# Masked graph attention with nodes on the partitions, and 32x32 squares crossed inside SBUF

## The chip, the cores and the metric

The kernel runs on one core of a Trainium2 chip. The metric is the device time of one execution, in microseconds (us). The kernel before takes 4419.53 us, the median of 3 runs (4417.87 to 4420.16 us). Engines are named as in the profile: PE is the matrix engine (PEld its weight loads), DVE the vector engine, ACT the activation engine, POOL the general one, SP the engine whose queue issues nearly all DMAs.

## The reference

There are 32 independent graphs. Each has x of 512 nodes by 256 features, and all share one adjacency matrix `adj` (512x512, about 0.8% ones). Four layers follow each other, each of the form `x = x + layer(relu(layernorm(x)), adj)`:

- Layer 0: a matrix 256->512, an attention without mask over 512 features, a matrix 512->256, then **masked attention** over 256 features, with ELUs and residuals between.
- Layer 1: **masked attention** over 256 features; the mask also holds the diagonal.
- Layer 2: ordinary multi-head attention (MHA), 8 heads of 32 features, masked, then two layer norms and two 256x256 matrices.
- Layer 3: **masked attention** with 4 heads of 64 features.

The masked attention of layers 0, 1 and 3 is, cut to what matters:

```python
f1 = h @ a[:F];  f2 = h @ a[F:]                  # one number per node
e = leaky_relu(f1[:, None] + f2[None, :], 0.2)    # (512, 512)
e = where(adj > 0, e, -9e15)
out = elu(softmax(e, axis=1) @ h)
```

So one graph needs six 512x512 masked tables of this kind (layer 0: one, layer 1: one, layer 3: four) and eight of the MHA's kind.

## The kernel before, in words

All data are fp32. A [512, 256] array lies in SBUF as [128 partitions, 4, 256]; such a "cell" is 4 KB a partition. The program is not written in the order in which it runs. For each graph, `Graph` records operations (`op`, `transfer`) with an engine, a planned length and the buffers read and written. `Plan.order` then schedules all graphs' operations in a list: at each step it takes the engine that can start first, and there the operation with the smallest due time. Due times come from `PERIOD`, `CLOSE` and the list `SHIFTS`, one entry for each operation counted from the graph's end. Up to `IN_FLIGHT = 6` graphs are open at once. Buffers (32 cells, 7 rows, 48 DRAM pages, 12 DRAM sheets, 8 PSUM banks) are given out by the same list. The result is one fixed order for each engine, and one for the SP queue, which issues every DMA of the steady state: a DMA whose input is late holds up the DMAs behind it.

The parts that matter here:

- **`gat_probabilities` (L776)** makes one masked table with the *sources* on the partitions, so that PE can use it as it is. For each table: `rows_ps` (L714, the PE work on L720) spreads a column of node numbers over all partitions by four 128x128 transposes into a PSUM bank. This happens three times (f2, w, f1). DVE takes the greatest masked f2 of each node (four of L791); four short POOL operations (L806 to L809) make w from it; ACT copies w's row out of PSUM (L730); POOL adds the mask to it in two halves (L821); DVE takes the greater of f1 and a term and adds (four of L832); ACT takes the exponential (four of L840).
- **`lonely` and `spread` (L846, L867)** give nodes without a neighbour the mean of all nodes: POOL sums, one PE product with a matrix of ones (L859), an ACT copy (L863), a POOL product (L870).
- **`attended` (L918)** multiplies a table with the node features (PE, L927) and divides by the row sums on DVE (L944 to L951).
- **`layer3` (L1450)** builds four tables, sums them over sources with POOL (L1484, L1488) and PE (L1523), multiplies with PE (L1502), turns the results and the sums back (L1539), and adds the lonely nodes' mean on POOL (L1572).
- **`mha` (L1329)** already has its nodes on the partitions. Its products (L1347), mask and maximum (L1367), exponentials with their sums (L1378) make tables that must be transposed. DVE turns every 32x32 square in place (L1386). Then the squares change places: one DMA of 1 MB writes them to a DRAM sheet (L1391) and four DMAs of 256 KB, each to 32 partitions, read them back (L1399). PE reads the result in runs of 32 numbers (L1412). Table and crossed table are each a `Quad`, four neighbouring cells.
- **`turned_round` (L631)** transposes a layer's normalized input the same way (two DVE operations on L636, then L615 and L622 through a DRAM page); layers 0 and 2 use it. **`transposed` (L647)** does it on PE with eight transposes (L655) and two ACT copies (L663); layers 1 and 3 use it, and the second half of layer 2.

Of the kernel before, what the change touches and what calls it, by code (L numbers as in the profile page):

```python
# [9 lines left out]
FP = mybir.dt.float32  # L10
I32 = mybir.dt.int32
BF = mybir.dt.bfloat16
# [24 lines left out]
TERMS = 3  # L37
MOST = 40.0

FLOOR = -(2.0**60)  # L40
TINY = 1e-30
# [3 lines left out]
CELL = NC * (C + 5)  # L45
ROW = N + 10
SMALL = 320
BUFFERS = {"cell": 32, "row": 7, "page": 48, "sheet": 12}
# [6 lines left out]
PERIOD = 50.7  # L55
CLOSE = 1.0

SHIFTS = (
    72, 50, 37, 26, 40, 30, 9, 57, 9, 9, 9, 9, 50, 27, -10, -39, 3, -6, 21, -19, -30, -122,
    -182, -23, -9, -33, 39, 5, -2, 1, -49, 1, 1, 0, -66, 1, 1, 1, 1, -16, 1, -38, -1, -71, -1,  # L60
    0, -23, 1, 2, -22, 1, 3, 1, -103, 1, 5, 1, -19, 1, 1, 19, 1, -26, 1, -3, 1, 1, 1, 14, 5, 0,
    1, 1, -10, 1, -2, 0, 0, 0, 1, 0, -1, 0, -1, 6, 0, -115, 19, 0, 7, -25, -6, 0, -32, -35, 0,
    68, 0, 35, 0, 93, -3, 2, 24, -51, 18, -11, 0, -7, 1, -75, 1, 1, 55, 0, 26, -26, 4, 3, 0,
    -39, -1, -162, -3, -56, -2, -13, 1, -20, -2, -37, -87, -26, -9, -7, -1, -27, -9, -52, -40,
    6, -52, -18, 0, -6, -4, 2, -5, -23, -88, 0, -14, -42, 12, -11, -1, -2, 6, -7, -10, -1, -49,
    -29, -3, -1, -23, 2, 0, -84, 10, -16, -46, -3, 7, 7, -17, 0, 0, 0, 0, -18, 0, 4, 144, 2, 0,
    -3, 0, -7, 2, -24, 27, -28, 31, -92, 47, -25, -10, 1, 0, -3, 0, 109, 0, -1, -75, -1, 0, 0,
    -3, 0, -7, -45, 0, 41, -1, 2, -7, 69, -15, -49, -3, -3, 0, 22, -97, -17, 4, -12, -9, 4, -53,
    -11, -1, -1, -5, 17, 5, 72, 47, 46, 74, 146, -16, -51, 41, -3, -13, -15, 2, 0, 1, 49, -18,
    -5, 30, 3, 4, 0, 0, -1, 0, 18, 14, -12, -32, 78, -1, 37, -82, -4, 7, -6, 0, 9, -3, -12, 9,  # L70
    0, -70, 20, 0, -10, 0, -1, 0, 23, 0, 0, -33, -10, 28, 83, 95, 37, 17, 76, -5, -36, -119,
    -25, -1, 92, 3, 0, 2, -3, 0, -24, 1, 0, -10, -5, -3, -36, -2, -46, -24, -68, 25, -10, -11,
    -13, -5, -2, -29, -22, -1, -1, -13, -2, 3, 14, 0, 0, 0, 28, 7, -83, -101, 7, 46, -9, -54,
    -46, 44, -24, 99, -5, -1, 0, 0, 75, 0, 0, 0, -10, 0, 1, 6, 0, 14, 0, 23, 13, -17, 53, 6, 87,
    -7, -16, 7, 3, 5, -1, -71, -87, 15, -12, 0, 11, 0, 0, 0, 8, 0, 0, -9, -8, 0, 23, 0, 0, -80,
    2, 0, 18, 0, 0, -3, 0, 0, 105, -13, -36, -11, -81, -30, -85, -143, -51, -24, -71, -29, -116,
    -48, -84, -82, -187, -154, -123, -175, -94, -43, -87, -62, 6, -91, -111, -160, -332, -388,
    -421, -351, -608, -395, -425, -396, -421, -341, -408, -335, -348, -464, -413, -372, -375,
    -378, -330, -297, -285, -312, -291, -315, -190, -199, -193, -90, -130, -236, -99, 76, -225,
    -189, -251, -299, -395, -387, -220, -242, -187, -183, -124, -28, -137, -109, -189, -108,  # L80
    -163, -117, -33, -55, -60, -125, -183, -244, -216, -176, -221, -264, -255, -199, -296, -271,
    -259, -434, -424, -521, -444, -340, -233, -214, -298, -180, -115, -52, -68, -145, -240,
    -205, -240, -241, -326, -236, -241, -474, -309, -46, -175, -128, -162, -177, -202, -326,
    -320, -212, -315, -229, -218, -238, -255, -252, -253, -294, -281, -196, -99, -190, 0, -59,
    -31, 0, -31, 3, -6, 2, 0, 2, -13, 0, 0, 0, 0, 16, 0, 141, -61, 0, 0, 0, -77, -2, -15, -29,
    -84, -35, -22, -60, -26, -26, -15, -26, -229, -39, -46, -103, -103, -16, -128, -41, -4, -61,
    -7, 35, -2, -9, 23, 3, 2, -22, -73, 5, -12, 2, 2, 2, -6, 2, 2, -5, 3, 2, 64, -18, 3, -11, 3,
    -24, 2, 2, 2, 3, 3, 42, 3, 1, 3, -26, 1, 3, -80, 17, -29, 27, -4, 3, 3, 3, 3, 3, 3, 3, -42,
    3, 0, -10, -36, -8, -69, -213, 23, -10, -20, 25, 26, 33, -18, 68, -12, -53, 17, 91, 94, 5,
    111, 25, 57, 164,  # L90
# [46 lines left out]
class Quad(Buffer):  # L137

    width = 4

    def __init__(self, *shape):
        super().__init__("cell", *shape)
# [266 lines left out]
def adj_preln_kernel(  # L409
# [35 lines left out]
    ident_bf = const.tile([P, P], BF, name="ident_bf")  # L445
    nc.vector.tensor_copy(ident_bf, ident)
    ones = const.tile([P, P], FP, name="ones")
# [5 lines left out]
    tiny = const.tile([P, NC], FP, name="tiny")  # L453
    nc.vector.memset(tiny, TINY)
# [20 lines left out]
    def row(v, name):  # L475
# [6 lines left out]
    mask_biasT = const.tile([P, NC, N], BF, name="mask_biasT")  # L482
    self_biasT = const.tile([P, NC, N], BF, name="self_biasT")
    alone = const.tile([P, NC], FP, name="alone")
# [5 lines left out]
    hand_sb = weights(W_hand, "hand_sb", TERMS)  # L490
    l1_sb = weights(W_1, "l1_sb", TERMS)
# [4 lines left out]
    l3_sb = weights(W_3, "l3_sb", TERMS * GAT_HEADS)  # L496
# [10 lines left out]
    none = const.tile([P, NC], FP, name="none")  # L507
# [8 lines left out]
    cells = work.tile([P, BUFFERS["cell"] * CELL], FP, name="cells")  # L516
    Buffer.at["cell"] = [cells[:, k * CELL :] for k in range(BUFFERS["cell"])]
    Buffer.at["bank"] = banks
    Buffer.at["sheet"] = [
        pages.tile([P, QUAD], FP, name=f"sheet{k}") for k in range(BUFFERS["sheet"])  # L520
    ]
    Buffer.at["page"] = [
        pages.tile([P, PAGE], FP, name=f"page{k}") for k in range(BUFFERS["page"])
    ]
    smalls = [work.tile([P, SMALL], FP, name=f"smalls{k}") for k in range(IN_FLIGHT)]
    masked = work.tile([P, N], FP, name="masked")
# [14 lines left out]
    out_v = out.rearrange("b (c p) f -> b p c f", p=P)  # L541

    class Graph:
# [129 lines left out]
        def channels_first(self, src, w, cols, dst, bias=None):  # L673

            nk = w.shape[1]
            for m in range(2 * len(dst)):
# [12 lines left out]

                def emit(m=m, mm=mm, d=d, i=i):  # L690
                    if bias is None:
                        act.activation(d[:, i, :], mm.ap, AF.Copy)
                    else:
                        act.activation(d[:, i, :], mm.ap, AF.Relu, bias=bias[:, m : m + 1])
# [81 lines left out]
        def gat_probabilities(self, holder, term, n, bias, biasT, own=False, after=()):  # L776

            f2_ps = self.rows_ps(holder, lambda c: term(0)[:, c : c + 1], after)

            top = self.small(f"top{n}", NC)
            w = self.small(f"w{n}", NC)
            for c in range(NC):
                self.op(
                    "dve", 0.77, [f2_ps, held("mask", c)], [top],  # L790
                    lambda c=c: dve.tensor_tensor_reduce(  # L791
                        masked, f2_ps.ap, bias[:, c, :], 1.0 - ALPHA, FLOOR,
                        op0=ALU.add, op1=ALU.max, accum_out=top[:, c : c + 1],
                    ),
                )
            if own:
                self.op(
                    "dve", 0.25, [top, *holder], [top],
                    lambda: dve.scalar_tensor_tensor(
                        top.ap, term(2), -1.0, top.ap, op0=ALU.mult, op1=ALU.max  # L800
                    ),
                )

            def emit():
                t = top.ap
                pool.tensor_add(w.ap, t, term(1))  # L806
                pool.tensor_scalar(w.ap, w.ap, 0.0, -1.0, op0=ALU.max, op1=ALU.mult)
                pool.tensor_scalar(t, t, -ALPHA / (1.0 - ALPHA), None, op0=ALU.mult)
                pool.tensor_add(w.ap, w.ap, t)  # L809

            self.op("pool", 1.0, [top, *holder], [top, w], emit)
            p = [Buffer("cell", 2, N) for _ in range(2)]
            w_row = self.row_of(w, lambda c: w[:, c : c + 1], p)

            def bias_key(half):
                return [("selfT" if own else "maskT", 2 * half + i) for i in range(2)]

            for half in range(2):
                self.op(
                    "pool", 2.17, [w_row, bias_key(half)], [p[half]],  # L820
                    lambda half=half: pool.tensor_add(  # L821
                        p[half].ap,
                        biasT[:, 2 * half : 2 * half + 2, :],
                        w_row[:, None, :].to_broadcast([P, 2, N]),
                    ),
                )
            f1_ps = self.rows_ps(holder, lambda c: term(1)[:, c : c + 1], [w_row])
            for j in range(NC):
                ph, i = p[j // 2], j % 2
                self.op(  # L830
                    "dve", 0.75, [f1_ps, *holder, ph.part(i)], [ph.part(i)],
                    lambda j=j, ph=ph, i=i: dve.scalar_tensor_tensor(  # L832
                        ph[:, i, :], f1_ps.ap, term(2)[:, j : j + 1],
                        ph[:, i, :],
# [813 lines left out]
```

## Time and profile before

| quantity | value |
|---|---|
| median of the runs | 4419.53 us |
| the profiled execution's own time | 4422.42 us |
| its span, first to last instruction | 4420.6 us |
| mean granted PE clock | 0.979 |
| PE busy over the span | 4170.8 us (94%) |
| DVE, POOL, ACT busy | 3662.7, 3034.1, 2924.3 us |
| DMA moved, mean busy share of the 16 DMA engines | 867.22 MB, 66.4% on SP's queue |

The profile has several views. The page gives busy times over the span. A table by stage gives the same for a stretch of time: for each engine its busy us and, in brackets, the number of its instructions, then PE's granted clock, the DMA engines' busy share and the GB/s moved. The groups give for one line of the code the shapes, the count, the busy us, the mean ns of one instruction, and the idle time before them with what ended it. The timeline lists instructions in order: start, us, engine, line, shapes, count. Instructions of one engine overlap at their ends, so the time that one more instruction costs is the distance between starts, a little less than its duration.

### The profile page before, as it was taken

How to read it: one execution, taken by the hardware profiler on the slowest of the kernel's cores; microseconds unless marked ns; L12 is line 12 of the kernel's file. 1: busy time of each engine (PE TensorE's matmuls, PEld its weight loads, DVE VectorE, ACT ScalarE, POOL GpSimd, SP SyncE). 2: the span in 40 equal slices, each digit the busy share in tenths (PEclk: the TensorE clock that was granted, in tenths of full speed). 3: DMA queues.
4: the chain of work that ended last, by engine and by line, in shares of the span. 5: the costliest groups of instructions: out<-in, count | busy, mean ns of one | idle time of the engine just before them, and what ended most of it. 6: DMA issues, size and time to landing. Idle time of an engine off the chain costs nothing. (4 is left out here: it accounts for less than half of the span.)

```text
span 4420.6 us, 69315 instructions
## 1 busy us (share of the span) xinstructions
PE 4170.8 (94%) x21648; PEld 2583.3 (58%) x21648; DVE 3662.7 (83%) x9016; ACT 2924.3 (66%) x6309; POOL 3034.1 (69%) x3119
## 2 busy tenths in 40 slices
PE   6999999999999999999999999999999999999765
PEld 3656556665566666566666556666656666655332
DVE  3577888888888888888888888888889888888873
ACT  2556666777676667667667767666766766676653
POOL 1424766777776677776677777667777766777677
PEclk9999999999999999999999999999999999999877
DMA  3287667766767766766777667677667677766760
GB/s 121 84 226 218 187 190 220 218 202 181 215 199 211 224 200 201 204 204 194 222 215 204 201 200 211 194 224 210 205 205 206 192 217 219 201 200 186 231 175 29
DMA packets 441504, 867.22 MB, mean 196 GB/s; under 512 B 35248, under 2 KB 119728, under 8 KB 441136
## 3 DMA queue, kind: packets, MB, share of 16 engines
q1 hardware_dynamic: 439520, 862.78, 66.4%
q8 instruction: 173, 2.83, 0.3%
q14 instruction: 195, 1.60, 0.1%
q10 hardware_dynamic: 1616, 0.01, 0.0%
HBM read 443.23 MB, written 419.43 MB: 195 GB/s over the span
## 5 line engine op out<-in xcount | busy, mean ns | idle before, releaser
L1386 DVE STREAM_TRANSPOSE cells<-cells 128x512 f32<-128x512 f32 x1024 | 702.4, 698 | 148.8 <-ACT cells L1378 148.5
L1378 ACT ACTIVATE cells<-cells,smalls 128x512 f32<-128x512 f32 x1024 | 736.1, 719 | 114.0 <-DVE smalls L1367 105.8
L1367 DVE CUSTOM_DVE_ANT_0 cells<-bank,mask_bias 128x512 f32<-128x512 f32 x1024 | 686.9, 674 | 21.6 <-PE bank L1347 20.6
L821 POOL TENSOR_TENSOR cells<-mask_biasT,row 128x1024 f32<-128x1024 bf16 x320 | 682.3, 2155 | 16.2 <-ACT row L730 16.2
L791 DVE CUSTOM_DVE_ANT_0 masked<-bank,mask_bias 128x512 f32<-128x512 f32 x768 | 520.5, 678 | 71.1 <-PE bank L720 64.7
L683 PE MATMUL bank<-cells,mlp_sb 128*128 128x512 f32 x1024 | 473.1, 600 | 19.8 <-DMA cells<-page 13.2
L704 PE MATMUL bank<-fc_sb,cells 128*128 128x256 f32 (+1 forms) x2048 | 474.7, 381 | 1.5 <-DVE smalls L1367 0.8
L927 PE MATMUL bank<-cells 128*128 128x260 f32 x2048 | 465.1, 383 | 1.1 <-ACT cells L840 0.9
L603 ACT ACTIVATE cells<-cells,smalls 128x256 f32<-128x256 f32 x768 | 408.1, 592 | 74.7 <-POOL smalls L596 49.7
L1159 PE MATMUL bank<-cells 128*128 128x512 f32 x1024 | 450.9, 597 | 0.0
L927 PEld LDWEIGHTS bank<-cells 128*128 128x128 f32 x2048 | 387.9, 190 | 87.1 <-issue 24.9
L840 ACT ACTIVATE cells<-cells,smalls 128x512 f32<-128x512 f32 x512 | 348.5, 726 | 114.7 <-DVE cells L832 114.6
L704 PEld LDWEIGHTS bank<-fc_sb,cells 128*128 128x128 f32 x2048 | 376.9, 189 | 76.5 <-DVE cells L1442 19.0
L586 DVE BATCH_NORM_STATS2 smalls<-cells 128x6 f32<-128x256 f32 x768 | 311.3, 405 | 110.4 <-POOL cells L1222 101.3
L883 ACT ACTIVATE cells<-cells 128x512 f32<-128x512 f32 (+1 forms) x256 | 188.1, 735 | 292.9 <-DVE cells L946 111.3
L832 DVE SCALAR_TENSOR_TENSOR cells<-bank,smalls,cells 128x512 f32<-128x512 f32 x512 | 354.1, 740 | 30.5 <-POOL cells L821 27.0
L720 PEld LDWEIGHTS bank<-ident,smalls 128*128 128x128 f32 x2176 | 254.3, 141 | 212.6 <-issue 84.2
L720 PE MATMUL bank<-ident,smalls 128*128 128x128 f32 x2176 | 325.9, 284 | 54.2 <-POOL smalls L809 30.0
L1159 PEld LDWEIGHTS bank<-cells 128*128 128x128 f32 x1024 | 194.1, 193 | 230.2 <-issue 228.7
L1484 POOL TENSOR_TENSOR cells<-cells 128x1024 f32<-128x1024 f32 x128 | 302.3, 2372 | 19.2 <-PE bank L1502 8.4
L683 PEld LDWEIGHTS bank<-cells,mlp_sb 128*128 128x128 f32 x1024 | 186.0, 191 | 218.5 <-issue 170.3
L1347 PE MATMUL bank<-cells 32*128 32x512 f32 x2048 | 305.8, 644 | 5.7 <-DVE smalls L1367 4.8
(141 smaller groups left out, 8503.9 us busy)
## 6 DMA issues: line engine op xcount, KB each, us to landing
sheet<-cells SPq DMA_DIRECT2D x256, 1024.0 KB, 5.3
cells<-sheet SPq DMA_DIRECT2D x1024, 256.0 KB, 5.4
page<-cells SPq DMA_DIRECT2D x256, 512.0 KB, 3.4
cells<-page SPq DMA_DIRECT2D x192, 512.0 KB, 6.1
cells<-in_x_dram SPq DMA_DIRECT2D x64, 512.0 KB, 7.3
cells<-page SPq DMA_DIRECT2D x256, 128.0 KB, 2.9
out_dram<-cells SPq DMA_DIRECT2D x32, 512.0 KB, 5.4
mlp_sb<-in_L_gnn_mlp_w_dram SPq DMA_DIRECT2D x2, 512.0 KB, 6.7
```

Source lines behind the costliest of these rows:

```text
L603: lambda c=c: act.activation(xn[:, c, :], src[:, c, :], func, bias=off[:, c : c + 1], scale=rstd[:, c : c + 1],),
L683: lambda k=k, s=s, i=i, m=m, mm=mm: pe.matmul(mm.ap, w[:, k, cols + m * P : cols + (m + 1) * P], s.rows(i), start=(k == 0), stop=(k == nk ...
L704: pe.matmul(mm[:, :n], src[k // 2].nodes(k % 2, c), w[:, k, cols : cols + n], start=(k == 0), stop=(k == nk - 1),)
L720: pe.transpose(bc[:, c * P : (c + 1) * P], col(c).to_broadcast([P, P]), ident)
L791: lambda c=c: dve.tensor_tensor_reduce(masked, f2_ps.ap, bias[:, c, :], 1.0 - ALPHA, FLOOR, op0=ALU.add, op1=ALU.max, accum_out=top[:, c : ...
L821: lambda half=half: pool.tensor_add(p[half].ap, biasT[:, 2 * half : 2 * half + 2, :], w_row[:, None, :].to_broadcast([P, 2, N]),),
L832: lambda j=j, ph=ph, i=i: dve.scalar_tensor_tensor(ph[:, i, :], f1_ps.ap, term(2)[:, j : j + 1], ph[:, i, :], op0=ALU.max, op1=ALU.add,),
L927: pe.matmul(mm[:, :w1], p[j // 2][:, j % 2, c * P : (c + 1) * P], v[:, j, :], start=(j == 0), stop=(j == NC - 1),)
L1159: pe.matmul(mm.ap, h1[jh][:, i, m * P : (m + 1) * P], p[jh][:, i, :], start=(jh + i == 0), stop=(jh + i == 2),)
L1367: dve.tensor_tensor_reduce(tile(), sc[h].ap.rearrange("p (j f) -> p j f", j=NC), mask_bias[:, c, :].rearrange("p (j f) -> p j f", j=NC), - ...
L1378: lambda h=h, c=c, tile=tile: act.activation(tile(), tile(), AF.Exp, scale=-1.0, bias=low[:, c, h : h + 1], accum_out=sums[:, c, h : h + 1],),
L1386: dve.transpose(squared, squared)
```

## The change

All masked tables are now made with the *targets* on the partitions, as the MHA's are, and turned by DVE and DMA:

- `masked_probabilities` takes the place of `gat_probabilities`. One spread row for each table instead of three. DVE adds the mask and takes the maximum, writing the table itself. One POOL addition and two small ACT operations make the shift. ACT applies the leaky slope as one instruction (`Prelu` with a bias), then the exponential; in layer 3 the exponential also gives the row sums. DVE turns the squares.
- `squares_crossed` moves each of the 16 blocks of squares with a DMA of its own from SBUF to SBUF, 128 KB (layer 3, and MHA in the same manner) or 64 KB (layers 0 and 1), each from 32 partitions to 32 partitions. Sheets in DRAM are gone.
- Layers 1 and 3 use `turned_round`. The nodes then come in an order by squares; the mask table is kept in that order, ACT writes r2T of layer 0 in that order, POOL copies it back to the plain one, and layer 3 fetches its residual and stores its result by quarters.
- `lonely`, `spread` and POOL's sums of layer 3 are gone; the divisions of `attended` become a DVE reciprocal and an ACT scaling.
- Quads get 5 buffers of their own beside 16 cells; rows go from 7 to 3. `PERIOD`, `CLOSE` and `SHIFTS` have other values.

```diff
-BUFFERS = {"cell": 32, "row": 7, "page": 48, "sheet": 12}
+BUFFERS = {"quad": 5, "cell": 16, "row": 3, "page": 48}
-PERIOD = 50.7
-CLOSE = 1.0
+PERIOD = 46.6
+CLOSE = 0.96
...
+        def masked_probabilities(self, holder, far, near, n, table, p, tile, parts, sums=None):
+            f2_ps = self.square_row(holder, far, [p])
...
+            for c in range(NC):
+                self.op("dve", 0.77, ...,
+                    lambda c=c: dve.tensor_tensor_reduce(
+                        tile(c), f2_ps.ap..., bias[:, c, :]..., 1.0, LOWEST,
+                        op0=ALU.add, op1=ALU.max, accum_out=top[:, c : c + 1]))
+            self.op("pool", 0.35, ..., lambda: pool.tensor_add(top.ap, top.ap, near()))
+            def emit():
+                act.activation(m.ap, top.ap, AF.Prelu, alpha=ALPHA)
+                act.activation(m.ap, m.ap, AF.Copy, scale=-1.0)
+            self.op("act", 0.45, [top], [m], emit)
+            for c in range(NC):
+                self.op("act", 0.72, ..., lambda c=c: act.activation(
+                    tile(c), tile(c), AF.Prelu, bias=near()[:, c : c + 1], alpha=ALPHA))
+            for c in range(NC):
+                ... act.activation(tile(c), tile(c), AF.Exp, bias=m[:, c : c + 1], **out)
+                ... dve.transpose(squared, squared)
...
+        def squares_crossed(self, src, dst, read, write, kbytes):
+            for turn in range(squares):
+                for l in range(squares):
+                    to = (l + turn) % squares
+                    ... nc.sync.dma_start(
+                            dst(slice(to * SQUARE, (to + 1) * SQUARE), l),
+                            src(slice(l * SQUARE, (l + 1) * SQUARE), to))
+                    self.transfer([read], write(l, to), kbytes, emit, True)
...
         def attended(self, p, v, y):
-                        dve.reciprocal(rinv.ap, mm[:, C + TERMS : w1])
-                        dve.tensor_mul(y[:, c, :], mm[:, :C], rinv.ap.to_broadcast([P, C]))
+                    lambda mm=mm, rinv=rinv: dve.reciprocal(rinv.ap, mm[:, C + PAIR : w1]),
+                    ... act.activation(y[:, c, :], mm[:, :C], AF.Copy, scale=rinv.ap)
...
         def layer0(self):
-            self.channels_first(yT, mlp2_sb, 0, [r2T], bias=mlp2_bc)
+            self.channels_first(yT, mlp2_sb, 0, [r2T], bias=mlp2_bc, squares=True)
+            rows = Buffer("cell", KC, N)
+                ... pool.tensor_copy(rows[:, k, :]..., r2T[:, k, :]...)
+            q = self.masked_attention(h2, (mask_square, "square"), 1)
-            self.spread(self.lonely(h2, self.W1), z)
...
         def layer1(self):
-            hT = self.transposed(xn)
+            hT = self.turned_round(xn)
...
         def mha(self, g, qT, kT, v, y):
-                    self.transfer([parts], [[(sheet, c % 2)]], 1024, ...)
-                    for to in range(squares):
-                        self.transfer([[(sheet, c % 2)]], [[(pT, c % 2, to)]], 256, emit, True)
+                for turn in range(squares):
+                    for l in range(squares):
+                        to = (l + turn) % squares
+                        self.transfer([squared], [[(pT, l, to)]], 128, emit, True)
...
         def layer3(self):
-            hT = self.transposed(xn)
+            hT = self.turned_round(xn)
...
-                    self.op("pool", 2.4, p, [halves], ... pool.tensor_add ...)
-                    self.op("pool", 1.27, [halves], [total.part(i)], ... pool.tensor_add ...)
+                    self.masked_probabilities(...)
+                self.squares_crossed(..., 128)
-            self.op("pe", 0.94, sums, [acc, r], emit)
-            back = turned(r, [])
...
-            self.transfer([res], [], 512, lambda: nc.sync.dma_start(out_v[i], res.ap))
+            for q in range(P // SQUARE):
+                self.transfer([res], [], 128, lambda q=q: nc.sync.dma_start(
+                    rows_v[q], res[q * SQUARE : (q + 1) * SQUARE]))
```

In the MHA the 16 transfers of a pair of blocks wait for all eight tables of the pair; before, the sheet of each block left as soon as its four tables were done.

## The prediction

> **What bounds the kernel now.** I read the table by stage first: start, one stretch of the middle, end.
>
> ```profile
> core 0: us, PE busy (x) PEld busy (x) DVE busy (x) ACT busy (x) POOL busy (x), PEclk, DMA share, GB/s
> 0.00:110.00 110.00, 70.94 (x234) 43.42 (x235) 36.12 (x127) 28.15 (x51) 19.84 (x31) 0.97 0.39 121
> 1390.00:1520.00 130.00, 128.33 (x678) 79.73 (x677) 113.82 (x279) 90.69 (x197) 94.90 (x98) 1.00 0.70 206
> 4090.00:4421.00 331.00, 215.87 (x1090) 113.98 (x1090) 217.75 (x532) 169.78 (x357) 238.76 (x234) 0.80 0.50 145
> ```
>
> The timeline repeats every 130 us in the middle (L1159 starts at 1264.02 and 1393.35; SP's pattern comes back after 519.93 us, four graphs). So the middle row is one graph: PE is busy 128.33 of 130 us, DVE 113.82, POOL 94.90, ACT 90.69. **PE is the bound.** 32 x 130 = 4160 us; the other 260.6 us of the span are filling and draining. In the last stretch PE idles 115 us and POOL is the busiest.
>
> What one PE instruction costs I read from starts in PE's timeline:
>
> ```profile
> 2459.60 0.60 PE L720 MATMUL bank<-ident,smalls 128*128 128x128 f32 x4
> 2460.04 0.60 PE L859 MATMUL bank<-row,ones 128*128 128x256 f32 x2
> 2460.47 1.89 PE L1319 MATMUL bank<-qkv_sb,cells 128*128 128x256 f32 x8
> ```
>
> Four transposes last 0.60 us, but the next starts after 0.44. Multiplying the groups' mean (284 ns) would cost a block at 1.14 us and overstate the saving 2.6 times.
>
> **PE, for each graph.** Six tables lose two of three spread rows: 12 x 0.44 = 5.3 us. Two inputs are no longer turned by PE (four blocks, L655): 1.8. The two products with ones (L859): 0.9. Layer 3's sums (L1523, eight instructions, planned 0.94): 0.9, and their turn (L1539): 0.4. PE stands still 1.1 us before L1523 (24.1 us in 21 graphs of the middle), which goes too. Sum 10.4: **130 becomes 119.6 us**. The matrix products stay: layer 3's now read runs of 32 numbers, as L1412 does in the MHA, whose 32 instructions take 1.93 us for a computed 16 x 256 / 4 columns, at L683's pace 1.75, so nothing is added.
>
> **ACT.** These are the rows that I price with:
>
> ```profile
> L1378 ACT ACTIVATE cells<-cells,smalls 128x512 f32<-128x512 f32 x1024 | 736.1, 719 | 114.0 <-DVE smalls L1367 105.8
> L840 ACT ACTIVATE cells<-cells,smalls 128x512 f32<-128x512 f32 x512 | 348.5, 726 | 114.7 <-DVE cells L832 114.6
> L603 ACT ACT_TABLE_LOAD x1 | 1.3, 1283 | 5.3 <-DMA cells<-in_x_dram 5.3
> ```
>
> 24 leaky slopes of 128x512 are added. L840's starts lie 0.61 to 0.69 us apart in runs, so 14.6 to 16.7; I take 15.6. Sums read out in layer 3: 16 x 0.10 = 1.6. Twelve small ones at 0.21: 2.5. Eight scalings out of PSUM at 0.38 (L1112): 3.0. Gone are seven row copies (0.59), four of L663 (0.58), two of L863: -7.2. Sum 90.7 + 15.5 = **106 us**. No row shows the leaky slope. The single table load of the program, although Relu, Exp, Copy and Identity alternate, speaks for zero loads; a load at each change would be at least 2 x 6 x 1.28 = 15.4 us a graph, at most 48 x 1.28 = 61. I take 0, the nearest row. "ScalarE: Activation LUTs", section "Table sets: the hidden batching unit", names relu, copy, identity and abs as functions in every set, but not the leaky one; read strictly it would put ACT at 122 us or more.
>
> **DVE.** The mask and maximum stay (0.68 each); 24 of L832 (0.740) become 24 square turns (0.698): -1.0. Four turns of inputs: +2.8. `attended` loses L944 to L951 (116.2 us in the middle's 21.5 graphs, 5.4) and gains eight reciprocals of 0.16 (+1.2). Sum **111 us**. That eight tables are written in runs of 32 I cost at nothing, as L636 (690 ns) turns such runs no slower than L1386 (698); if they took twice as long, +5.4. ACT's two writes of r2T in square order likewise: nothing, or +1.4.
>
> **POOL** loses the mask additions (12 x 2.15), sums (15.0 in layer 3, 4.0 in `lonely`), spreading and adding means (6.7), and most small ones (6.1 to 1.3); it gains a copy (2.6): 94.9 to **41 us**. It was not the bound, so only the end gains.
>
> **DMA and SP.** Bytes do not change: before 8 + 8 MB through the sheets and 9.5 others; after 8 (MHA), 4 (layer 3), 2 (layers 0, 1) crossing, and 11.5 others. What changes is their kind. The DMA columns of two-us stretches (the last two numbers of each row):
>
> ```profile
> 2510.00:2512.00 2.00, 1.16 (x9) 0.32 (x10) 1.95 (x6) 0.00 (x0) 0.00 (x0) 1.00 1.08 213
> 2618.00:2620.00 2.00, 2.00 (x12) 0.59 (x9) 2.00 (x6) 1.79 (x5) 2.00 (x2) 1.00 1.04 398
> ```
>
> In the first, sheets are read into 32 partitions: the engines are full at 213 GB/s (199 to 222 beside it). In the second a 128-partition write runs at 398 (373 elsewhere). Checked on before: (8+1) MB at 213 is 44 us, 17.5 million bytes at 385 are 46, together 90 of 130 us, as the 0.70 says. No row shows SBUF to SBUF. If the 32 partitions set its pace as above: 17.8 million bytes (14.7 crossing, 3.1 other quarters) at 213 is 84 us, the rest 23, **107 us**. If full rate: 76. If reading and writing add up: 176. I take 107, the nearest row.
>
> "DMA: Bandwidth & Descriptors", section "Where 436 GB/s comes from", lets SBUF-to-SBUF run at the fabric's 435; "SBUF — State Buffer", section "Can I just issue two DMAs to hit both halves?", says that two DMAs on different halves serialize, and gives 32 partitions some 218. The second speaks against this change and is the one that our sheets agree with. By the first the crossing's 14.7 million bytes would take an estimated 34 us, by the second 67.
>
> SP issues 65 DMAs for a graph now, 169 after. One costs 0.43 us:
>
> ```profile
> L1399 SPq DMA_DIRECT2D cells<-sheet x1024: 302/430/2255, 226.8 to 4289.9; - x171
> ```
>
> 169 x 0.43 = 73 us of the period, 28 before. A crossing of 16 takes 6.9 us to issue and, at 213, 9.8 us to move. SP's added waits are for the last of eight turned tables (L1386); behind them in the queue stand other graphs' loads, and PE waits for those. PE's products of layers 0 and 1 (now L927) wait for squares instead of for ACT (L840); behind them in PE's order stand other graphs' products, and with six graphs open the order can place them late enough. The wait for the sheet to land (691 us of SP in all) disappears.
>
> At the start the mask makes one more trip through DRAM (about 3.4 us out, 2.9 back by L615's and L622's landings); the first masked table comes only after layer 0's first half, so this is covered; uncovered it costs 7 us once.
>
> **Buffers.** A quad pair is held for filling (MHA blocks leave SP 10 to 35 us apart), 10 us crossing, 3 landing and the products: some 50 us. Six pairs and two single ones are 390 quad-us of 5 x 121 a graph, so 64%: they should not stop the order, but leave little slack.
>
> **The sum.** After, PE has 119.6, DVE 111, DMA 107, ACT 106, SP 73. PE lost 1.7 us a period when the next engine had 12% to spare; now there is 7%, so I allow 2 us more: **121.5 us**. 32 x 121.5 = 3888, plus 260.6, less 10 for POOL's part in the end (L821 and L1484 fill a third of the last chain, but the crossings come in): span 4139. The profiled run is 1.8 us over its span and 2.9 over the median; forecast **4138 us**.
>
> **Rivals.**
> - *Tangle* (25%): four resources within 13% of each other and one fixed order; late DMAs stop PE for 4 to 6 us a period. 126 x 32 + 260 = 4292. For: DMA busy rises from 70 to 88%. Against: PE lost only 1.7 us with DVE at 88%.
> - *Better* (14%): order keeps PE as full as before and the end shortens by 30 without POOL's chain: 119.6 x 32 + 230 = 4057.
> - *The crossings become the bound* (7%): place, SP's queue and the 32-partition transfers. DMA is idle 39 us a period now, largely because SP stands before a semaphore (1002.7 us at L1391). If 30 of these remain beside 107 busy, the period is 137: 4644, **slower**. It decides at 130, so from 23 us of idle on, or, with 39, from a crossing rate below 14.7 million bytes / 53 us = 277 GB/s. Against: 691 us of SP's waits go.
> - *The leaky slope isn't free* (3%): table loads as priced, ACT 122 to 167: 4170 to 5600.
>
> **Chances.** PE stays the bound as forecast 50%, tangle 25, better 14, crossings 7, slope 3, other 1. Two in ten may be left out: the range runs from 4040 to 4340, over the first three cases. Differences under 0.2% (9 us) cannot be told from none. Faster 0.90, same 0.02, slower 0.08.
>
> **What would show it.** Right: L720's successor has 36 instructions a graph, the middle repeats at 120 to 123 us with PE 97% busy, DMA at 0.85 to 0.90 and near 215 GB/s in crossings, one table load. Wrong: PE under 95% with waits on DMA (tangle or crossings), crossings near 390 GB/s (my DMA sum too high), DVE or ACT over 115 us.

## The result: 11% slower, and the profile after

The changed kernel takes **4918.95 us**, the median of 4 runs (4916.12 to 4940.13 us); the kernel before took 4419.84 beside it. The ratio is 1.1138 (95% interval 1.1106 to 1.1170). The forecast was 4138 us, the range ended at 4340, and "slower" had a chance of 0.08.

The table by stage of the changed kernel, with one period of the middle and the same lengths at both ends as were shown of before:

```profile
core 0: us, PE busy (x) PEld busy (x) DVE busy (x) ACT busy (x) POOL busy (x), PEclk, DMA share, GB/s
0.00:110.00 110.00, 68.99 (x223) 42.70 (x224) 34.84 (x117) 28.61 (x54) 19.07 (x32) 0.97 0.43 131
2507.91:2654.61 146.70, 124.72 (x583) 72.75 (x582) 105.65 (x263) 102.37 (x238) 41.89 (x53) 0.93 0.70 183
4585.00:4916.00 331.00, 168.56 (x800) 84.29 (x800) 188.08 (x482) 180.80 (x442) 70.92 (x93) 0.73 0.59 147
```

The start is as before. In the middle SP's pattern repeats after 146.70 us (2507.91 to 2654.61) where a graph took 130. No engine is full any more: PE is busy 85% of the period, under the 95% that the prediction named as a sign of being wrong, and DVE, ACT and POOL have 105.65, 102.37 and 41.89 us, close to the forecast 111, 106 and 41. **The work on the engines came out as forecast; the time is idle time.** 32 x 16.7 us are 534 us more; filling and draining take 222 us where they took 260.6 (4916.0 - 32 x 146.7), so 39 less: 495 in sum, as measured between the two spans (4916.0 and 4420.6).

Who waits for what comes from the groups, from the records of one line, and from the page's list of DMA issues:

```profile
L1410 SPq DMA_DIRECT2D quad<-quad x2048: 507/589/1987, 231.8 to 4769.6; - x187
```

```profile
quad<-quad SPq DMA_DIRECT2D x3072, 128.0 KB, 2.4
...
quad<-quad SPq DMA_DIRECT2D x1024, 64.0 KB, 2.0
```

L1410 is the MHA's crossing, L858 that of layers 0, 1 and 3. The three numbers after the colon are least, median and greatest duration in ns: SP needs 589 ns for one issue where a read of a sheet needed 430 (L1399 before). There are 128 such issues in a graph. PE's product of layers 0 and 1 shows the other end of it, before (L927) and after (L935; the last numbers are the idle time ahead of it and what ended most of that):

```profile
L927 PE MATMUL bank<-cells 128*128 128x260 f32 x2048 | 465.1, 383 | 1.1 <-ACT cells L840 0.9
L935 PE MATMUL bank<-cell,quad 128*128 128x259 f32 x2048 | 549.4, 426 | 188.1 <-DMA quad<-quad 101.4
```

The timeline of one period shows them beside the work that waits (the number in square brackets is the idle time ahead of an instruction):

```profile
2545.44 21.73 SPq L858 DMA_DIRECT2D quad<-quad  x32
...
2554.24 3.67 PE L935 MATMUL bank<-cell,quad 128*128 128x259 f32 x16
...
2567.23 0.69 DVE L807 CUSTOM_DVE_ANT_0 quad<-bank,mask_square 128x512 f32<-128x512 f32 x1 [3.52 <-DMA quad<-quad]
...
2568.09 6.43 PE L935 MATMUL bank<-cell,quad 128*128 128x259 f32 x16 [4.65 <-DMA quad<-quad]
...
2574.55 10.14 SPq L1410 DMA_DIRECT2D quad<-quad  x16
```

16 issues take 10.14 us, 0.63 us each, and two crossings that come together hold the queue for 21.73 us. PE's product L935 then stands 4.65 us until squares land that it reads, and DVE's next table (L807) waits 3.52 us for a quad that the crossing uses. Added over this one period, SP's records are 43.42 us (L1410), 42.96 (L858) and 21.5 for the 41 other DMAs: **108 us of issuing in a period of 146.7**; the rest of SP's time is waits in front of DMAs whose input is not ready.

The second row of L935 shows a second loss. The 16 instructions took 6.43 us where they take 3.67. The table in steps of two us tells why (third number from the end: PE's granted clock):

```profile
2562.00:2564.00 2.00, 1.31 (x10) 1.07 (x10) 1.71 (x4) 2.00 (x6) 0.79 (x1) 0.83 0.95 219
2564.00:2566.00 2.00, 0.00 (x0) 0.00 (x0) 0.00 (x0) 1.34 (x3) 1.92 (x3) 0.50 0.84 193
...
2568.00:2570.00 2.00, 1.91 (x5) 1.56 (x6) 1.16 (x4) 2.00 (x4) 0.39 (x1) 0.50 0.91 291
2570.00:2572.00 2.00, 2.00 (x6) 1.62 (x5) 0.08 (x1) 0.53 (x1) 0.00 (x0) 0.50 0.84 294
2572.00:2574.00 2.00, 2.00 (x7) 1.56 (x7) 1.30 (x5) 0.72 (x1) 1.44 (x2) 0.61 0.75 214
2574.00:2576.00 2.00, 2.00 (x11) 0.74 (x11) 1.44 (x6) 1.24 (x3) 0.21 (x1) 1.00 0.16 37
```

PE has worked only 2.0 of the 4.7 us before it comes to stand at 2563.44; the clock falls to 0.50 just there, and it is full again only some 5 us after PE is back at work at 2568.09. This wait is paid for twice.

### The profile page after: what moved, and what is told of

Its sections match the earlier page's. It is cut to its first block, busy times and chain, and to the rows that moved or that the text cites. A ratio compares the mean times of both kernels' runs of the same rounds, so it can differ in the third digit from the quotient of the medians.

```text
span 4916.0 us, 67801 instructions
## 1 busy us (share of the span) xinstructions
PE 4071.5 (83%) x19072; PEld 2412.9 (49%) x19072; DVE 3485.8 (71%) x8715; ACT 3352.7 (68%) x7809; POOL 1328.5 (27%) x1711
## 5 line engine op out<-in xcount | busy, mean ns | idle before, releaser
L1393 ACT ACTIVATE quad<-quad,smalls 128x512 f32<-128x512 f32 x1024 | 732.6, 716 | 265.7 <-DVE smalls L1382 223.5
L1401 DVE STREAM_TRANSPOSE quad<-quad 128x512 f32<-128x512 f32 x1024 | 692.0, 694 | 69.2 <-ACT quad L1393 64.9
L1382 DVE CUSTOM_DVE_ANT_0 quad<-bank,mask_bias 128x512 f32<-128x512 f32 x1024 | 676.8, 666 | 73.4 <-PE bank L1362 51.8
L935 PE MATMUL bank<-cell,quad 128*128 128x259 f32 x2048 | 549.4, 426 | 188.1 <-DMA quad<-quad 101.4
L846 DVE STREAM_TRANSPOSE quad<-quad 128x512 f32<-128x512 f32 x768 | 509.8, 692 | 128.5 <-ACT quad L837 126.5
L935 PEld LDWEIGHTS bank<-cell,quad 128*128 128x128 f32 x2048 | 427.0, 213 | 320.5 <-issue 87.2
L601 ACT ACTIVATE cell<-cell,smalls 128x256 f32<-128x256 f32 x768 | 422.4, 593 | 173.9 <-DMA page<-cell 88.6
L837 ACT ACTIVATE quad<-quad,smalls 128x512 f32<-128x512 f32 x768 | 527.8, 711 | 0.9
L681 PE MATMUL bank<-cell,mlp_sb 128*128 128x512 f32 x1024 | 486.7, 607 | 45.1 <-DMA cell<-page 39.1
L807 DVE CUSTOM_DVE_ANT_0 quad<-bank,mask_square 128x512 f32<-128x512 f32 x640 | 416.3, 675 | 141.8 <-DMA quad<-quad 67.8
L711 PE MATMUL bank<-fc_sb,cell 128*128 128x256 f32 (+1 forms) x2048 | 480.2, 389 | 39.6 <-DVE smalls L1382 36.9
L1169 PE MATMUL bank<-cell,cell 128*128 128x512 f32 x1024 | 454.0, 596 | 0.0
L1509 PE MATMUL bank<-quad,cell 128*64 128x512 f32 x1024 | 274.9, 685 | 171.9 <-DMA quad<-quad 114.2
L829 ACT ACTIVATE quad<-quad,smalls 128x512 f32<-128x512 f32 x512 | 354.6, 712 | 58.8 <-issue 46.2
```

The source lines that it names most:

```text
L601: lambda c=c: act.activation(xn[:, c, :], src[:, c, :], func, bias=off[:, c : c + 1], scale=rstd[:, c : c + 1],),
L681: lambda k=k, s=s, i=i, m=m, mm=mm: pe.matmul(mm.ap, w[:, k, cols + m * P : cols + (m + 1) * P], s.rows(i), start=(k == 0), stop=(k == nk ...
L711: pe.matmul(mm[:, :n], src[k // 2].nodes(k % 2, c), w[:, k, cols : cols + n], start=(k == 0), stop=(k == nk - 1),)
L807: lambda c=c: dve.tensor_tensor_reduce(tile(c), f2_ps.ap.rearrange("p (a i) -> p a i", i=tile(c).shape[2]), bias[:, c, :].rearrange("p (a ...
L837: act.activation(tile(c), tile(c), AF.Exp, bias=m[:, c : c + 1], **out)
L846: dve.transpose(squared, squared)
```

## The experiments

Four theories were on trial. **A, issue**: the number of DMAs in SP's queue. **B, pace**: the bytes, moved at the pace of 32 partitions. **C, order**: the planned list and the five quads. **D**: the crossings by issue and pace together. Each time is compared with the kernel before on the same chip.

**Halving the issues.** Eight DMAs of 64 partitions in place of 16 of 32, the same bytes. Squares land in wrong places, so the masked attentions are not the reference's.

```diff
-    dst(slice(to * SQUARE, (to + 1) * SQUARE), l), src(slice(l * SQUARE, (l + 1) * SQUARE), to)
+    if to % 2 == 0: return
+    half = to // 2; other = (half + l) % 2
+    dst(slice(half * 64, half * 64 + 64), l), src(slice(other * 64, other * 64 + 64), l)
```

> The changed kernel with every crossing made by 8 DMAs of 64 partitions instead of 16 of 32: the same bytes, the order of all other work unchanged, 64 issues fewer on SP for a graph. The squares land in other places than they should, so the result is not the reference's. Theory A (issue): SP's queue paces the kernel, because one SBUF-to-SBUF DMA takes SP 0.62 us, 128 of them 79 us of the 147 us period, beside 18 us for the other DMAs and 45 us of waits; 40 us fewer let PE be the bound again, period 122 to 130 us, 4170 to 4430 us. Theory B (pace): the transfers themselves are slow since 32 partitions only carry some 210 GB/s; if 64 partitions carry no more, 4850 to 4950 us. Theory C (order): the planned order and the five quads set the pace; 4800 to 4920 us.

Measured: 4631.23 us, ratio 1.0467 (1.0437 to 1.0497), in none of the three ranges. 288 us of the 499 are gone with unchanged bytes. The DMAs hardly became faster: beside such crossings the profile shows 215 to 238 GB/s (199 to 219 in the changed kernel). Each issue became dearer, 8 in 7.36 us (0.92 each), so SP's time for a crossing fell by a quarter only:

```profile
2561.37 7.36 SPq L1418 DMA_DIRECT2D quad<-quad  x8
...
2562.00:2564.00 2.00, 2.00 (x10) 0.67 (x7) 1.97 (x7) 1.97 (x6) 0.82 (x3) 1.00 1.04 238
```

**Halving the bytes.** All 16 DMAs, each with the first half of its row; the other half of the receiving table keeps other values.

```diff
+    n = a.shape[1] // 2
+    nc.sync.dma_start(a[:, :n], b[:, :n])
```

> The changed kernel with every crossing DMA moving only the first half of its row: the same number of issues, 7 MB fewer for a graph. Half of each crossed table is then old data, so the result is not the reference's. Theory A (issue): at least 4800 us, as SP issues as many. Theory B (pace): the crossings take 34 us less of DMA time, 4300 to 4600 us. Theory C (order): 4800 to 4920 us.

Measured: 4709.16 us, ratio 1.0643 (1.0612 to 1.0674): 210 us less, between the ranges of A and B. 16 issues still took 10.12 us. So bytes count too, and neither theory alone is enough.

**One small transfer.** The crossings of MHA and layer 3 become one DMA each, of 16 KB by the profile's list (`quad<-quad SPq DMA_DIRECT2D x192, 16.0 KB, 1.9`; the expectation says 64), so these two attentions are computed from other values; layers 0 and 1 keep theirs.

```diff
+    if (l, to) != (3, 2): return
+    pT[:16, 0]...[:, :, :32], p[:16, 0]...[:, :, :32]
```

> The changed kernel, its order unchanged, with the 16 crossing DMAs of each MHA pair and of each layer-3 pair replaced by one DMA of 16 partitions and 128-byte runs (64 KB); layers 0 and 1 cross as before. 90 DMAs and 12 MB fewer for a graph; most of each crossed table is old data, so the result is not the reference's. It is the ceiling of what the crossings cost. Theory D (crossings, issue and pace together): PE is the bound again, 122 to 126 us a graph, 4120 to 4300 us, PE clock at 0.97 or more. Theory C (order and five quads): the planned order and the buffers cost most of the loss, 4500 to 4650 us. Theory A or B alone can't be told apart here.

Measured: 4254.21 us, ratio 0.9623 (0.9594 to 0.9652). Its table by stage:

```profile
1000.00:2000.00 1000.00, 959.66 (x4769) 576.38 (x4768) 860.93 (x2158) 827.55 (x1950) 330.39 (x424) 0.99 0.37 115
```

PE is at 96% and a graph follows the other every 126 us (by the starts of the loads of x from 1000 to 4000 us). So the slope on ACT, the runs of 32, the reciprocals and the POOL work cost nothing that was not forecast; 665 us hang on these crossings. It is still 116 us above the forecast.

**Few issues with all bytes, and all issues with few bytes.** This pair splits the 665 us. First, four DMAs of 128 partitions and 512 KB for each crossing of MHA and layer 3; the squares stay on their own partitions, so these attentions get wrong weights:

```diff
+    if to != 0: return
+    pT[:, l]..., p[:, l]...
```

> The crossings of MHA and of layer 3 go as 4 transfers of 128 partitions and 512 KB in place of 16 of 32 partitions and 128 KB, in the places of four of the sixteen in the planned order: the same bytes, a quarter of the issues. The squares stay on their own partitions, so these two attentions get wrong weights; layers 0 and 1 are as in the changed kernel. Theory A (each issue holds SP's queue for about 0.6 us, and 96 of the 128 issues of a graph are these): 24 issues remain in place of 96, so nearly all that one small transfer a crossing won (4919 to 4254) is won here too, 4250 to 4350. Theory B (the bytes themselves, at the 199 to 219 GB/s that the windows show while crossings run, are what the readers wait for): the bytes are unchanged, so 4700 or more, unless transfers of 128 partitions are faster than those of 32, which the windows beside them will show.

Second, all 16 DMAs, each with an eighth of the row:

```diff
+    n = a.shape[1] // 8 if kbytes == 128 else a.shape[1]
+    nc.sync.dma_start(a[:, :n], b[:, :n])
```

> The crossings of MHA and of layer 3 keep their 16 transfers of 32 partitions, but each carries the first eighth of a row, 16 KB in place of 128 KB; the rest of the receiving tile keeps what stood there, so these two attentions are computed from partly old values. Layers 0 and 1 are as in the changed kernel. Theory A (issue): all 128 issues of a graph remain, so it stays at 4600 or more, hardly below the 4709 of half the bytes. Theory B (bytes): nearly what one small transfer a crossing gave, 4254 to 4350. If both count and add up, the step from all to half of the bytes (210 us) goes on in a straight line: 4919 less 1.75 x 210, 4550.

Measured: the first 4289.48 us, ratio 0.9702 (0.9684 to 0.9720); the second 4665.22 us, ratio 1.0556 (1.0538 to 1.0575); both lie in the ranges of theory A. Their rows of the table by stage, the first kernel's, then the second's, and then the changed kernel's:

```profile
1000.00:4000.00 3000.00, 2849.42 (x14069) 1710.05 (x14066) 2556.95 (x6398) 2459.91 (x5785) 968.24 (x1246) 0.98 0.62 212
```

```profile
1000.00:4000.00 3000.00, 2680.11 (x12873) 1602.15 (x12872) 2333.98 (x5837) 2255.16 (x5273) 891.50 (x1143) 0.96 0.38 115
```

```profile
1000.00:4000.00 3000.00, 2573.55 (x12125) 1526.86 (x12124) 2199.78 (x5476) 2112.39 (x4946) 839.43 (x1070) 0.94 0.69 182
```

The first moves 212 GB/s and keeps PE at 95%; the second moves 115, its DMA engines idle for 62% of the time, and PE is at 89%. With few bytes the issue is as long as ever, as the second kernel's timeline shows:

```profile
2176.35 10.02 SPq L1413 DMA_DIRECT2D quad<-quad  x16
```

**In this order the number of issues is the larger part.** Of the 665 us, 411 stay when all issues are made and carry an eighth of the bytes (4665 against 4254), and 254 come with the bytes. Over the middle the period is 127 us in the first kernel, 139 in the second and 147 in the changed kernel (by the same starts as above): 12 us a graph and 8. The first kernel's bytes are cheap for one more reason. Where such a crossing runs, the profile shows

```profile
2041.00:2043.00 2.00, 2.00 (x11) 1.73 (x10) 1.92 (x6) 0.82 (x3) 0.00 (x0) 1.00 1.01 404
2043.00:2045.00 2.00, 2.00 (x8) 1.18 (x7) 1.80 (x8) 0.63 (x3) 0.00 (x0) 1.00 1.03 412
```

that is 404 to 412 GB/s with 128 partitions, against 199 to 219 in the changed kernel's crossings of 32:

```profile
2578.00:2580.00 2.00, 2.00 (x7) 1.01 (x6) 0.58 (x1) 1.78 (x7) 1.26 (x1) 1.00 0.97 215
2584.00:2586.00 2.00, 2.00 (x10) 1.66 (x9) 1.84 (x6) 2.00 (x6) 0.74 (x3) 1.00 0.88 199
```

"DMA: Bandwidth & Descriptors", section "Where 436 GB/s comes from", of the Trainium skill, with 435 for SBUF to SBUF, fits the first; its page "SBUF — State Buffer" (section "Door 1: The DMA port swizzle (why `[64,N]` ≈ `[32,N]`)"), with some 218 for 32 partitions, fits the second. The second has a rival, though: one 128 KB piece every 0.63 us is 208 GB/s at most, so the issues alone would allow no more. The engines' share of 0.88 to 0.97 says that both limits lie close together here. So this run alone would not split count from bytes; the second kernel does, with issues and partitions unchanged.

**Another queue.** The crossings of layers 0, 1 and 3 are issued by POOL, which is busy 27% of the span; the list is unchanged.

```diff
-    nc.sync.dma_start(
+    nc.gpsimd.dma_start(
```

> The changed kernel with the 64 crossing DMAs of layers 0, 1 and 3 issued from POOL's queue, which is idle 73% of the time, and the MHA's 64 from SP as now. Theory A (issue): SP loses 40 us of issue for a graph; 4200 to 4600 us unless an issue on POOL takes over 1.5 us (64 of them then fill its idle 107 us). Theory B (pace) and theory C (order): 4850 to 4950 us.

Measured: 5069.75 us, ratio 1.1458 (1.1422 to 1.1495), slower still and in none of the ranges. One group of its page tells what happened:

```profile
L858 POOL DMA_DIRECT2D quad<-quad x2048 | 1017.1, 502 | 450.6 <-DVE quad L846 144.4
```

POOL issues one in 0.50 us, but it too works in order: it stands 450.6 us before these DMAs, and what POOL has behind them stands with it. PE's wait for squares at L935 rises from 101 to 224 us in all. Taking issues off SP does not help if another in-order queue must wait for the same tables.

**The price in the plan, alone.** The list is made with 0.58 us for a crossing issue in place of 0.45, with the same `PERIOD`, `CLOSE` and `SHIFTS`.

```diff
-    self.op("sp", 0.45, reads, writes, emit)
+    self.op("sp", issue, reads, writes, emit)      # 0.58 for crossings
```

> The changed kernel with the planner told that a crossing DMA takes SP 0.58 us instead of 0.45 (the trace has 0.589), so the order is made anew. Theory A (issue) with an order that knew too little: 4500 to 4800 us. If SP's time itself is the bound whatever the order: 4850 to 5000 us. Theory C (order): an order made for other lengths moves the time either way by some per cent.

Measured: 5181.48 us, ratio 1.1720 (1.1684 to 1.1757). The plan itself now ended at 4837 us: due times that fit one set of lengths do not fit another. The run says how delicate the list is and nothing of the price.

**The price in the plan, with due times searched for it.** Crossing issues at 0.62 us, and new `PERIOD` (47.07), `CLOSE` (1.0008) and `SHIFTS`, from a search over the list's own rules; nothing else differs.

> The same work, the same DMAs and the same buffers as the changed kernel; only the order of the list is another. The plan is told that a crossing issue holds SP for 0.62 us (the measured pace in a run) in place of 0.45, and PERIOD, CLOSE and SHIFTS are searched anew for this price; the plan then ends at 4408 us by its own prices (the changed kernel's ended at 4205 with 0.45, and its order at 4673 when each crossing issue is priced at 0.62). If the loss is that the order was planned with too low a price of an issue, and issues alone matter, 4420 to 4500. If the bytes' pace counts beside it (the new order ends at 4580 when crossings also move at 213 GB/s in place of the planned 290), 4550 to 4650. If the order hardly matters and SP's hundred us for a graph are simply too many, 4800 to 4920, as the changed kernel.

Measured: 4728.68 us, ratio 1.0702 (1.0681 to 1.0723). It lies between two expectations: 190 us come back by order alone, more than "order hardly matters" allows and less than the other two. To see what holds the rest, the same order was run with an eighth of the bytes, by the edit already shown:

> The kernel with the order planned anew (4728.68 us), and its transfers of MHA and layer 3 carry the first eighth of each row, 16 KB in place of 128 KB, so these two attentions are computed from partly old values; the number of issues and the order are unchanged. If what is left between that order's own plan (4408 us) and its time is the bytes' pace, 4420 to 4480. If it is the number of issues, whose price the plan has but whose waits it misjudges, 4650 or more. In the old order the same edit took 254 us (4919 to 4665); if both do their part as there, about 4500 to 4550.

Measured: 4474.73 us, ratio 1.0122 (1.0101 to 1.0144), in the first of its three cases: 67 us above what this order's plan promises. The two edits add up: the order takes 190 us with all bytes (4919 to 4729) and 190 with an eighth (4665 to 4475), the bytes 254 with either order. With the new order less is left for the number of issues: 220 us above one small transfer a crossing (which ran in the old order), where the old order had 411.

**One part of the change alone**, in two forms: the kernel before, with its old list, and the MHA's squares sent directly.

```diff
-    nc.sync.dma_start(sheet[:, :, c % 2, :], p[:, :, c % 2]...)
-    nc.sync.dma_start(pT[to * SQUARE : ..., :, c]..., sheet[:, to, c]...)
+    nc.sync.dma_start(pT[to * SQUARE : ..., l]..., p[l * SQUARE : ..., to]...)   # 16 for a pair of blocks
```

> The kernel before, in its own order, with one part of the change alone: the MHA's squares go from SBUF to SBUF in 16 DMAs for a pair of blocks, and the sheets are gone. SP's issue goes from 28 to some 50 us for a graph of 130. Theory A (issue): SP still has room, 4390 to 4500 us. Theory B (pace): 8 MB fewer move out and the crossing takes what the sheets' reading took, 4380 to 4440 us. Theory C (order): unchanged, 4400 to 4440 us. Above 4500 us, waits of SP's queue at the crossings cost by themselves.

> The kernel before with the MHA's squares going from SBUF to SBUF, as in the first trial of this part, but sent at the place in the order where the second sheet was written, so that the table's cells are still its own. Theory D (crossings): 38 us of issue for 18 and the wait for all eight tables; 4430 to 4560 us. Theory C (order): unchanged order, 4400 to 4450 us.

Measured: 4577.49 us, ratio 1.0346 (1.0316 to 1.0376), with the DMAs where the sheet was read; 5036.35 us, ratio 1.1392 (1.1359 to 1.1425), with them where the second block's sheet was written. Both are **inconclusive**. The old list lets the first block's buffer go once its sheet is written, and may turn the first block after the second, so some squares carry wrong tables and SP's queue stands for tables it should not need. The 459 us between them come with the place in the list, not with the crossing.

## Why the prediction was wrong, step by step

- **PE's work: right.** Forecast 119.6 us a graph. With few issues (four wide transfers) the measured value is 2849.42 / 3000 x 127 = 121 us. In the changed kernel the same instructions take 126 (2573.55 us of 1000 to 4000, by the same sum with 147): the clock is 0.94 there and 0.98 with few issues. L935 has a mean of 426 ns where L927 had 383. The prediction had no term for a clock that falls in waits.
- **ACT, DVE and POOL: right.** The leaky slope is an ordinary pass and loads no table:

```profile
L601 ACT ACT_TABLE_LOAD x1 | 1.3, 1283 | 5.3 <-DMA cell<-in_x_dram 5.3
...
L829 ACT ACTIVATE quad<-quad,smalls 128x512 f32<-128x512 f32 x512 | 354.6, 712 | 58.8 <-issue 46.2
```

  "ScalarE: Activation LUTs", section "Table sets: the hidden batching unit", of the Trainium skill does not list this function among those in every set; the one load of the whole program decides. Writing runs of 32 costs DVE nothing (L807: 675 ns).
- **DMA: right in pace, and not the bound.** 213 GB/s for the crossings was the nearest row, and 199 to 219 came (partly luck, since the price of an issue would allow no more than 208). The DMA engines are busy 0.69 x 146.7 = 101 us of the period (forecast 107). That they are not the bound does not make the bytes free: 254 us come with them.
- **SP: this term failed.** "One costs 0.43 us" was taken from a read from DRAM and used for a kind of DMA that the trace did not show. A crossing issue takes 0.63 in a run (median of one 0.59), so a crossing of 16 takes 10.1 us to issue and not 6.9, and SP issues for 108 us a period and not for 73. No bounds were put around this price, as was done for the pace beside it.
- **The sum: a second failure behind it.** The periods of the engines were compared by busy time, and SP at 73 of 121 seemed to have room. But a crossing is a latency: in the MHA and in layer 3 the last of 16 transfers releases the reader, and two crossings in a row hold the queue for 21.73 us. "With six graphs open the order can place them late enough" is what the waits refute for this order. These are PE's waits in the changed kernel, middle 3000 us (in total, times, longest):

```profile
PE bank L935 <- DMA quad<-quad: 71.5, 30, 5.0
PE bank L653 <- ACT cell L601: 49.5, 60, 2.1
PE bank L1425 <- ACT cell L1282: 46.3, 34, 4.3
PE bank L1425 <- DMA quad<-quad: 44.7, 15, 8.6
PE bank L935 <- DVE smalls L807: 42.4, 9, 6.1
PE bank L1509 <- DMA cell<-page: 36.6, 15, 4.6
```

  and these with few issues (four wide transfers):

```profile
PE bank L655 <- ACT cell L603: 49.0, 57, 2.1
PE bank L941 <- DMA quad<-quad: 25.5, 18, 11.2
PE bank L1452 <- ACT row L1444: 8.8, 10, 1.5
```

  L653 (L655 there) waits the same in both, 2.4 us a graph, so these crossings do not cause it; the kernel before has no such wait in its middle (its largest is the 24.1 us of L1523 that the prediction names), so it is a small part of the loss that the prediction did not see. The direct waits for squares are 71.5 + 44.7 + 15.3 (L1509) us, 6.4 a graph. One other leads back to crossings: L807, for which L935 waits, itself waits for quads in a crossing (67.8 us over the span). L1509's 36.6 us are for reads from DRAM that the same queue issues; with few issues it has no such wait. The rest was not followed back.
- **The order was right only for its own prices.** Its plan has 0.45 us for each issue. The same list laid out with 0.62 ends 468 us later (4673 against 4205), by arithmetic alone; an order made for 0.62 wins 190 us on the chip. The plan also moves all bytes at 290 GB/s (`RATE`), while the prediction itself took 213 for the crossings; it has no term for a list that is made for 290 and runs at 213. The order planned anew still has 290, and 254 of about 320 us between its plan (4408) and its time (4729) go with the bytes.
- **The rivals.** "The crossings become the bound" is the one that came, by the mechanism and at the place it names, at 7%, though its 4644 us are 275 too few. It decides from 23 us of idle beside 107 of busy DMA on, and was priced with 30 of the 39 us that the kernel before had. Measured are 101 busy and 46 idle: all the idle time stayed, where the prediction let most of it go with the sheets' waits. That "Tangle" (4292 us) is near the time with four wide transfers (4289 us) is a coincidence of numbers: that is another kernel.
- **What stays open.** Order (190 us) and bytes (254) are measured one by one and together. The new order with little left to move still takes 4475 us, 220 above one small transfer a crossing; the number of issues is what differs most between these two, but their orders differ as well, and whether a better order for 0.62 us exists is not settled. ACT's queue was not tried, nor a crossing by fewer transfers that puts the squares where they belong. No kernel that computes the whole reference came below the kernel before.

## What to carry to other kernels

Count the issues of a DMA scheme as a resource of its own, and price them with the kind of transfer that will be issued: here, in the order as it was planned, 16 pieces of a table cost more by their number (411 us) than by their bytes (254). When a row for that price is missing, bound it and ask what the late last piece holds up, since a queue that issues for 108 of 146.7 us can still set the end. Give a planned order the prices that the forecast uses: the list made with 0.45 us for an issue that takes 0.63 lost 190 us to one made with 0.62.

## What the runs showed of the hardware

- An issue on SP took 0.63 to 0.68 us in a run for SBUF to SBUF with 32 partitions (32 in 21.73 us), about the same whether it moved 128, 64 or 16 KB (16 in 10.14, 10.12 and 10.02 us); 0.92 with 64 partitions (8 in 7.36 us) and 0.80 with 128 (4 in 3.20 us). A read from DRAM to 32 partitions took 0.43 before (median). POOL issued one in 0.50.
- SBUF to SBUF moved 404 to 412 GB/s with 128 partitions and 215 to 238 with 64, with the DMA engines full (share 1.01 to 1.05), and 199 to 219 with 32, with a share of 0.87 to 0.97 while the issues came at 208 GB/s.
- PE's granted clock fell to 0.50 at the start of a wait of 4.65 us, after 4.7 us in which PE had worked 2.0, and came back some 5 us after PE's work did; the same 16 instructions took 6.43 us in place of 3.67.
